# Twelve gather buffers instead of eight, and a tile's second eight gathers asked for earlier, in the first attention step of a four-layer graph kernel

## The chip, the cores and the metric

The kernel runs on one core of one Trainium2 chip. The metric is the device time of one execution in microseconds; the median of three executions is 3159.19 us. The engines are named as in the profile: PE is TensorE, DVE is VectorE, ACT is ScalarE, POOL is GpSimd, SP is SyncE. Each has a queue of its own that it works through in order.

## The reference

There are four layers over one graph of N = 4096 nodes with 256 features. Only layer 1 is touched here. Per step it forms attention weights, keeps of each row the largest ones that hold 90% of the mass, and multiplies the rows with them:

```
for n in range(STEPS):                       # STEPS = 2
    A = _top_p_attention(Xa, W1, W2, W3)     # softmax(q @ k.T), the smallest set of
                                             # largest entries with mass 0.9, renormalized
    Xf = R @ Xf                              # R: adjacency + identity, rows normalized
    Xa = A @ Xa
    Z = Z + Xf @ U1[n].T + Xa @ U2[n].T
h = X + Z                                    # then a layer norm
```

The layers around it are matrix products of the adjacency matrix with the features, small weights, and a layer norm after each.

## The kernel before, in words

The rows are cut into 32 tiles of 128. In step 0 the attention rows are sharp: nearly all rows need at most `KEPT = 16` of their 4096 entries. So the kernel does not multiply with a dense attention matrix there. For each tile it finds the 16 largest logits of every row and their columns (`tops`, with FIND_INDEX8 in two rounds of eight, L530), works out their weights (`pick`), and then fetches for k = 0 to 15 the feature row that the k-th column names: `gather` (L669) takes a buffer `G` of 128 x 256 float32 and issues an indirect DMA on POOL's queue, which reads 128 rows of 1 KB from `x1_d` in HBM. PE multiplies each `G` with a diagonal matrix `dg` of the k-th weights and sums the 16 products in `acc_bank` (L761). Rows for which 16 entries are not enough are flagged; `flag` (L582) works out a slot for each and writes the row's number into a list in HBM, `list_d`, with an indirect DMA of 128 elements of 4 bytes, on POOL's queue too (L606). They are done again later, densely.

`run_step` runs three tiles at once. In iteration i, tile i (`st`) is multiplied and finished, tile i + 1 (`cd`) is searched and gathered, and tile i + 2 (`nxt`) gets its logits. The body of an iteration is `pieces`: eight groups g = 0 to 7, each with a piece of the logits (L414), two of the 16 gather products of tile i (L761), four matmuls each of two products with the adjacency (`neighbours`: L686 into `acc_r`, L696 into `nef_ps`), and at the end the operations that `run_step` put into `ops[g]` with `at(g, ...)`. In the kernel before, the gathers of a tile are asked for in two halves:

- k = 0 to 7 by `run_step`, one iteration ahead, at the ends of groups 4 to 7 (two in each);
- k = 8 to 15 by `pieces`, in the tile's own iteration: directly after the product with k, the gather k + 8 is asked for.

With eight buffers in rotation, gather number s of the whole sequence takes the buffer of gather s - 8, so it waits on POOL until PE has multiplied with that one. For k = 8 to 15 this is the product with k - 8 of the same tile; for k = 0 to 7 of the next tile it is the product with k + 8 of this one.

Also on POOL's queue are the loads of the other copy of the adjacency, `adjn8` (L692), two of 256 KB in an iteration, each waiting for the matmuls L696 of an earlier half.

The order of the instructions on an engine is not the order of the Python text. The framework's planner plays the program through with costs of its own, takes for each engine the first instruction in text order that is ready in that play, and fixes the order so found; it also puts in the waits. It can be seen in the trace: in an iteration's start PE runs the products L761 of groups 0 to 2 and only then the eight L686 of groups 0 and 1, since `acc_r` is one buffer and is read first by `r_end` (L705 on ACT, L706 on DVE, behind a FIND_INDEX8 of 4.42 us). And `adjn8`'s load for the next iteration stands on POOL ahead of gathers that come earlier in the text.

Of the kernel before, what the change touches and what calls it, by code (L numbers as in the profile page):

```python
# [11 lines left out]
F32 = mybir.dt.float32  # L12
# [12 lines left out]
P = 128  # L25
D = 256
# [17 lines left out]
KEPT = 16  # L44
# [12 lines left out]
def gnn_stack(ctx, tc, x, adjt, adjn, w0, b0, w1, w2t, w3t, u1t, u2t, ln_g, ln_b, w2, b2, w3, b3, out):  # L57
# [28 lines left out]
    def half(bank):  # L86
        turns[bank] ^= 1
        return (mm_bank if bank == "mm" else acc_bank)[:, turns[bank], :]
# [268 lines left out]
    with tc.tile_pool(name="l1", bufs=1, reuse_waits="tile") as l1:  # L357

        cur = {"late": False, "n": 0, "nef_done": False}
# [57 lines left out]
        def logits_in(l):  # L417

            nc.vector.memset(l[:, N:], -1.0)
            return l  # L420
# [20 lines left out]
        def sparse(st):  # L441

            return cur["n"] == 0 and st["tile"] is not None
# [224 lines left out]

        def gather(st, k):  # L669

            st["G"][k] = g = cur["w"].tile([P, D], F32, tag="G", name="G", bufs=8)
            nc.gpsimd.indirect_dma_start(  # L672
                out=g, out_offset=None, in_=x1_d, in_offset=bass.IndirectOffsetOnAxis(ap=st["at"][:, k : k + 1], axis=0))

# [24 lines left out]
        def r_acc(i):  # L699

            return ps_acc.tile([P, 512], F32, tag=("acc", "nef")[i % 2 if cur["nef_done"] else 0], name="acc_r", bufs=1)
# [21 lines left out]
        def pieces(n, st, nxt, ops, rs_now=()):  # L723


            G = GP
            few = st is not None and sparse(st)
            if st is not None:
                e = st["e"]
                acc_a = half("acc")  # L730
                if "xf" not in st:
                    fetch(n, st)
            with_r = st is not None and len(rs_now) > 0
            if with_r:
                i, = rs_now
                acc_r, pn = r_acc(i), None
                if n == 0:
                    pn = ps_acc.tile([P, 512], F32, tag="nef", name="nef_ps", bufs=1)
            ats = {}

            def turn(g):
                ps = ps_tr.tile([P, 4, P], F32, tag="tr", name="at_ps")
                for j in range(G):
                    nc.tensor.transpose(ps[:, j, :], e[:, (g * G + j) * P : (g * G + j + 1) * P], ident)  # L744
                at = cur["w"].tile([P, G, P], F32, tag="at", name="at", bufs=2)
                ats[g] = at
                nc.scalar.copy(at[:, :G, :], ps[:, :G, :])  # L747

            if st is not None and not few:
                turn(0)  # L750
            for g in range(NLC):
                if nxt is not None:
                    logits_chunk(nxt["e"], nxt["q"], g)
                if few:
                    per = KEPT // NLC
                    for k in range(g * per, (g + 1) * per):
                        if k % 4 == 0:
                            dg = cur["w"].tile([P, 4, P], F32, tag="at", name="dg", bufs=2)
                            nc.vector.tensor_mul(dg, ident[:, None, :].to_broadcast([P, 4, P]),
                                                 st["w"][:, k : k + 4, None].to_broadcast([P, 4, P]))  # L760
                        nc.tensor.matmul(acc_a, dg[:, k % 4, :], st["G"][k], start=(k == 0), stop=(k == KEPT - 1))  # L761
                        if k + 8 < KEPT:
                            gather(st, k + 8)
                elif st is not None:
                    if g + 1 < NLC:
                        turn(g + 1)
                    for j in range(G):
                        jt = g * G + j
                        nc.tensor.matmul(acc_a, ats[g][:, j, :], cur["xa"][:, jt, :], start=(jt == 0),  # L769
                                         stop=(jt == NT - 1))  # L770
                if with_r:
                    neighbours(n, i, g, acc_r, pn, cur["xf"])
                for f in ops.get(g, ()):
                    f()
            if st is None:
                for i in rs_now:
                    r_product(n, i, cur["xf"])
            else:
                xa_new = work.tile([P, D], F32, tag="xa_new", name="xa_new", bufs=1)
                nc.scalar.activation(xa_new, acc_a, AF.Copy, scale=st["sc"])  # L780
                if n + 1 < STEPS:
                    put(xa_d, st, xa_new)
                st["xa"] = xa_new
            if with_r:
                r_end(i, acc_r, pn)
# [9 lines left out]
        def fetch(n, st):  # L795

            i = st["tile"]
            for key, src in (("xf", xf_d), ("res", h_d if n else x1_d), ("x1", x1b_d)):
                if n == 0 and (key == "x1" or key == "res" and i is not None):
                    continue  # L800
                if i is None:
                    st[key] = gathered(src, st, key)
                else:
                    st[key] = work.tile([P, D], F32, tag=key, name=key, bufs=1)
                    nc.sync.dma_start(st[key], rows(src, i))
            if n == 0 and i is not None:
                st["res"] = cur["xa"][:, i, :]
# [136 lines left out]
        def run_step(n, es):  # L944
# [37 lines left out]
            for i in range(-2, NT):  # L982
                st = tiles.pop(i, None)
                cd = tiles.get(i + 1)
                nxt = None
                if i + 2 < NT:

                    nxt = {"tile": i + 2, "q": cur["qs"].pop(0), "e": logits_in(es[i % 2]), "later": later, "G": {}}
                    tiles[i + 2] = nxt
                if i + 1 == NT and n == 0:  # L990
                    for fs in last:
                        for f in fs:
                            f()
                    last = []
                    left_over(n, es[NT % 2], later)
                ops = {}

                def at(g, f, *args):
                    ops.setdefault(g, []).append(lambda: f(*args))

                for g, fs in zip((1, 2), last):
                    for f in fs:
                        at(g, f)
                if 0 < i + 2 < NT - 1:
                    turned = []
                    g = 1 if n else 6
                    at(g - 1, lambda i, turned: turned.append(transposed(cur["xa"][:, i + 3, :])), i, turned)
                    at(g, lambda turned: cur["qs"].append(query(None, turned[0])), turned)
                if cd is not None:
                    peak_groups(cd, NG_LATER if n else ngr)  # L1010
                    at(1, exp_rows, cd)
                for job in jobs:
                    at(1, advance, job)
                if cd is not None:
                    rounds = ROUNDS if n else KEPT // 8
                    at(2, tops, cd, rounds)
                    at(2, pick, cd, rounds)
                    at(4, flag, cd)
                    if n == 0:
                        for k in range(8):  # L1020
                            at(4 + k // 2, gather, cd, k)
                    else:
                        at(5, lambda cd: [None for _ in settle(cd)], cd)
                for job in jobs:
                    if n and i + 1 == NT:
                        at(4, advance, job)
                    at(6, advance, job)
                if i + 1 == NT and n == 0:
                    cur["next"] = load_halves(es[1 - NT % 2], xf_d, nc.sync)
                if i < 0:  # L1030
                    now = FIRST[n][i + 2]
                else:
                    now = [i + 2] if FIRST[n][1][-1] < i + 2 < NT else []
                pieces(n, st, nxt, ops, now)
                last = [[f] for f in after(n, st)] if st is not None else []
                if i in starts:
                    k = starts[i]
                    if len(jobs) > (i == NT - 2):
                        last = finish(jobs.pop(0), last)
                    e = es[NT % 2] if k + 1 == LATER[n] else es[2]  # L1040
                    jobs.append({"stages": put_off(n, k, e, later)})
                    if i < NT - 2:
                        advance(jobs[-1])
# [28 lines left out]
        for n in range(STEPS):  # L1072
            cur["n"] = n
            with tc.tile_pool(name=f"step{n}", bufs=2, reuse_waits="tile") as cur["w"], \
# [6 lines left out]
                else:  # L1081
# [3 lines left out]
                    for c in range(NLC):  # L1085
# [5 lines left out]
                        k = kS[:, c * LC : (c + 1) * LC].rearrange("p (j d) -> p j d", d=P)  # L1091
# [137 lines left out]
```

## Time and profile before

| | |
|---|---|
| median of three executions (lowest, highest) | 3159.19 us (3156.39, 3160.6) |
| the profiled execution, its own time | 3226.1 us |
| its span, from first to last instruction | 3224.4 us |
| mean granted PE clock | 0.967 |
| step 0, gathers on POOL | from 388 us to 1314 us of the span |
| PE busy, whole span | 2945.7 us (91%) |
| POOL busy, whole span | 778.7 us (24%) |
| DVE busy, whole span | 2260.9 us (70%) |
| gathers (L672) | 512, mean 974 ns on POOL |
| list writes (L606), 400 us to 1400 us | 32, mean 1230 ns on POOL |
| FIND_INDEX8 (L530) | 64, mean 4419 ns on DVE |

How to read it: the profiled execution is one execution and took 67 us (2.1%) longer than the median of the others, so a difference taken from the trace is set against 3226.1 us first and then carried over to 3159.19 us. Shares over the whole span mix stages: POOL's 24% is mostly step 0. [...]

### The profile page before, as it was taken

Reading aid. Unit: us, or ns where it says so; the run is one execution under the profiler, and the core shown is the slowest. Engines: PE = TensorE matmul, PEld = TensorE weight load, DVE = VectorE, ACT = ScalarE, POOL = GpSimd, SP = SyncE. Lnnn points to the kernel's source line nnn. Section 1 sums busy time; section 2 is a strip of 40 time slices with the busy share of each in tenths; the row PEclk is TensorE's granted clock in tenths of the full one; section 3 lists DMA queues with packets and bytes.
Section 4 is the critical chain, followed back from the end, with each engine's and each line's share of the span. In section 5 each row is a group of like instructions: output and inputs, shape, how many; then the busy total and the mean of one; then the engine's idle time right before and its main releaser. Section 6 shows DMA issues by size and latency. Waiting matters only on the chain. (4 is left out here: it accounts for less than half of the span.)

```text
span 3224.4 us, 45413 instructions
## 1 busy us (share of the span) xinstructions
PE 2945.7 (91%) x14244; PEld 2313.2 (72%) x14244; DVE 2260.9 (70%) x7159; ACT 1729.6 (54%) x2883; POOL 778.7 (24%) x908
## 2 busy tenths in 40 slices
PE   7999888999989997779998999999999986999998
PEld 3788666777767775567777787778887654777886
DVE  4666667778777776447998898986999654444444
ACT  3555545556555554545554655555555434666664
POOL 1121256666666665100000000010000100000000
PEclk9999988999999998889999999999999997999999
DMA  9995467777777776241000011111111234333332
GB/s 169 157 178 121 82 96 121 140 140 138 139 134 138 134 135 135 88 122 38 24 24 23 27 37 32 32 35 33 38 34 29 85 108 143 107 108 97 107 107 79
DMA packets 247484, 299.44 MB, mean 93 GB/s; under 512 B 34464, under 2 KB 201312, under 8 KB 247232
## 3 DMA queue, kind: packets, MB, share of 16 engines
q0 software_dynamic: 46336, 104.28, 23.5%
q1 hardware_dynamic: 188656, 180.93, 18.7%
q10 hardware_dynamic: 12240, 11.23, 1.1%
q8 instruction: 115, 1.88, 0.3%
q14 instruction: 137, 1.12, 0.2%
HBM read 330.65 MB, written 66.32 MB: 123 GB/s over the span
## 5 line engine op out<-in xcount | busy, mean ns | idle before, releaser
L686 PE MATMUL acc_r<-xh,adjq 128*128 128x512 f32 x2048 | 619.3, 431 | 31.5 <-ACT adjq L683 17.1
L769 PE MATMUL acc_bank<-xa,at 128*128 128x256 f32 x2240 | 548.7, 385 | 26.8 <-ACT at L747 26.4
L672 POOL DMA_INDIRECT G<-x_d,cols x512 | 498.5, 974 | 296.1 <-PE acc_bank L761 143.3
L683 ACT CAST adjq<-adj 128x512 fp32r<-128x512 fp8e4 x512 | 316.4, 620 | 431.4 <-PE acc_r L686 237.2
L769 PEld LDWEIGHTS acc_bank<-xa,at 128*128 128x128 f32 x2240 | 408.3, 192 | 85.9 <-ACT at L747 38.1
L686 PEld LDWEIGHTS acc_r<-xh,adjq 128*128 128x128 f32 x2048 | 379.4, 191 | 125.8 <-ACT adjq L683 38.3
L433 DVE MAX8 cand<-e 128x8 f32<-128x228 f32 (+1 forms) x1088 | 387.3, 402 | 81.2 <-ACT e L415 44.8
L415 ACT COPY e<-lg 128x512 f32<-128x512 f32 x544 | 315.7, 586 | 209.2 <-PE lg L414 172.6
L199 POOL TENSOR_TENSOR rstd<-ve,mhalf 128x1 f32<-128x1 f32 x166 | 100.5, 606 | 1334.2 <-DVE ve L197 1274.0
L414 PE MATMUL lg<-kS,q 128*128 128x512 f32 x1088 | 391.9, 445 | 9.8 <-issue 5.5
L1109 ACT CAST a<-a 128x1024 fp32r<-128x1024 fp8e4 x256 | 268.4, 1050 | 167.0 <-PE acc L175 127.8
L761 PE MATMUL acc_bank<-G,dg 128*128 128x256 f32 x1024 | 291.8, 405 | 46.8 <-DMA G<-x_d,cols 15.1
L530 DVE FIND_INDEX8 cols<-top,e 128x8 uint32<-128x4096 f32 x64 | 282.8, 4419 | 0.0
L175 PE MATMUL acc<-xh,a 128*128 128x512 f32 x1024 | 262.1, 410 | 20.0 <-DMA x2i<-x_d 16.2
L761 PEld LDWEIGHTS acc_bank<-G,dg 128*128 128x128 f32 x1024 | 199.5, 200 | 104.5 <-issue 23.4
L175 PE MATMUL acc<-y0h,a 128*128 128x512 f32 x1024 | 249.8, 397 | 0.0
L175 PEld LDWEIGHTS acc<-xh,a 128*128 128x128 f32 x1024 | 193.3, 192 | 67.5 <-ACT xh L151 21.7
L175 PE MATMUL acc<-yh,a 128*128 128x512 f32 x1024 | 237.9, 394 | 0.0
L175 PEld LDWEIGHTS acc<-yh,a 128*128 128x128 f32 x1024 | 192.1, 188 | 43.8
L175 PEld LDWEIGHTS acc<-y0h,a 128*128 128x128 f32 x1024 | 187.9, 188 | 38.9 <-issue 0.6
L747 ACT COPY at<-at_ps 128x512 f32<-128x512 f32 x288 | 168.9, 588 | 82.4 <-PE at_ps L744 79.6
L414 PEld LDWEIGHTS lg<-kS,q 128*128 128x128 f32 x1088 | 182.3, 195 | 32.4 <-ACT e L415 11.1
(287 smaller groups left out, 4447.1 us busy)
## 6 DMA issues: line engine op xcount, KB each, us to landing
adj<-adj_d SPq DMA_DIRECT2D x256, 128.0 KB
a<-adj_d SPq DMA_DIRECT2D x256, 128.0 KB
a<-in_adjt POOLq DMA_DIRECT2D x64, 256.0 KB
adj_d<-a SPq DMA_DIRECT2D x64, 256.0 KB
adjn<-in_adjn POOLq DMA_DIRECT2D x64, 256.0 KB
x_d<-x SPq DMA_DIRECT2D x64, 128.0 KB
xf_d<-xf_new SPq DMA_DIRECT2D x64, 128.0 KB
G<-x_d,cols POOLq DMA_INDIRECT x512
```

The source lines that it names most:

```text
L175: nc.tensor.matmul(acc, a[:, j, :], halves(jt), start=(jt == 0), stop=(jt == NT - 1))
L414: nc.tensor.matmul(pl[:, :LC], q[k], kS[:, s], start=(k == 0), stop=(k == 1))
L415: nc.scalar.copy(l[:, s], pl[:, :LC])
L433: nc.vector.max(dst[:, 8 * g : 8 * g + 8], src[:, g * w : min((g + 1) * w, N)])
L530: nc.vector.max_index(st["at"][:, 8 * r : 8 * r + 8], t8, st["e"][:, :N])
L672: nc.gpsimd.indirect_dma_start(out=g, out_offset=None, in_=x1_d, in_offset=bass.IndirectOffsetOnAxis(ap=st["at"][:, k : k + 1], axis=0))
L683: nc.scalar.copy(a, cur["a8"][:, g % 2 * GP : (g % 2 + 1) * GP, :])
L686: nc.tensor.matmul(acc_r, a[:, j, :], xf[:, jt, :], start=(jt == 0), stop=False)
L747: nc.scalar.copy(at[:, :G, :], ps[:, :G, :])
L761: nc.tensor.matmul(acc_a, dg[:, k % 4, :], st["G"][k], start=(k == 0), stop=(k == KEPT - 1))
L769: nc.tensor.matmul(acc_a, ats[g][:, j, :], cur["xa"][:, jt, :], start=(jt == 0), stop=(jt == NT - 1))
L1109: nc.scalar.copy(a, a8)
```

## The change

The buffers of `G` become twelve. The gathers k = 8 to 15 of a tile leave the loop of products in `pieces`; `run_step` asks for them with `at` at the ends of groups 0 to 3 of the tile's own iteration, two in each group. The number of gathers, what they read and what is computed stay as they are. With twelve buffers in rotation, gather s takes the buffer of gather s - 12.

```diff
         def gather(st, k):
 
-            st["G"][k] = g = cur["w"].tile([P, D], F32, tag="G", name="G", bufs=8)
+            st["G"][k] = g = cur["w"].tile([P, D], F32, tag="G", name="G", bufs=12)
             nc.gpsimd.indirect_dma_start(
                 out=g, out_offset=None, in_=x1_d, in_offset=bass.IndirectOffsetOnAxis(ap=st["at"][:, k : k + 1], axis=0))
...
                         nc.tensor.matmul(acc_a, dg[:, k % 4, :], st["G"][k], start=(k == 0), stop=(k == KEPT - 1))
-                        if k + 8 < KEPT:
-                            gather(st, k + 8)
...
                         at(5, lambda cd: [None for _ in settle(cd)], cd)
+                if n == 0 and st is not None:
+                    for k in range(8, KEPT):
+                        at(k // 2 - 4, gather, st, k)
                 for job in jobs:
```

## The prediction, made before the changed kernel was run

> **What bounds the kernel now.** I read the page's groups first, then the busy times of 100 us stretches, then the waits, then the timelines of two iterations. The chain that ended last is of no use here: it begins at 2665.92 us, long after step 0.
>
> ```profile
> L672 POOL DMA_INDIRECT G<-x_d,cols x512 | 498.5, 974 | 296.1 <-PE acc_bank L761 143.3
> L761 PE MATMUL acc_bank<-G,dg 128*128 128x256 f32 x1024 | 291.8, 405 | 46.8 <-DMA G<-x_d,cols 15.1
> ```
>
> POOL waits for PE to free buffers (143.3 us), and PE waits for gathered rows (15.1 us of 46.8): each waits for the other, so the buffers are short or something delays the rows. The stretches inside step 0, with columns as named in their first line:
>
> ```profile
> core 0: us, PE busy (x) PEld busy (x) DVE busy (x) ACT busy (x) POOL busy (x), PEclk, DMA share, GB/s
> 700.00:800.00 100.00, 92.14 (x512) 72.04 (x513) 81.48 (x242) 58.17 (x114) 66.18 (x70) 1.00 0.77 146
> 800.00:900.00 100.00, 91.04 (x492) 71.61 (x492) 77.27 (x214) 59.20 (x116) 65.96 (x69) 0.97 0.80 133
> ```
>
> PE is the fullest engine and idle 8 us in 100. POOL is fuller than it looks: behind each of its 69 instructions lie 0.30 us in which it waits for nothing shown, so it is taken for 66 + 21 = 87 us. The waits from 500 to 1230 us (in total, times, longest):
>
> ```profile
> PE nef_ps L696 <- DVE spare_row L710: 26.9, 17, 3.5
> PE acc_bank L761 <- DMA G<-x_d,cols: 10.4, 9, 2.1
> PE acc_bank L761 <- issue: 7.7, 14, 4.4
> ...
> POOL G L672 <- PE acc_bank L761: 108.1, 108, 3.2
> ```
>
> Now one iteration, POOL's timeline and then PE's:
>
> ```profile
> 825.99 0.95 POOL L672 DMA_INDIRECT G<-x_d,cols  x1 [0.65 <-PE acc_bank L761]
> 827.24 1.36 POOL L606 DMA_INDIRECT list_d<-ids,slots  x1 [0.31 <-issue]
> 828.91 0.96 POOL L672 DMA_INDIRECT G<-x_d,cols  x1 [0.30 <-issue]
> ...
> 837.08 0.98 POOL L672 DMA_INDIRECT G<-x_d,cols  x1 [0.30 <-DMA list_d<-ids,slots]
> ```
> ```profile
> 833.93 1.13 PE L761 MATMUL acc_bank<-G,dg 128*128 128x256 f32 x4 [0.16 <-issue]
> ...
> 837.34 0.70 PE L761 MATMUL acc_bank<-G,dg 128*128 128x256 f32 x2 [1.11 <-DMA G<-x_d,cols]
> ```
>
> Counting the products L761 (two records each), 833.93 is k = 0 and 1 and 837.34 is k = 3. On POOL 825.99 is k = 2 of that tile, then comes the list write, then k = 3 at 828.91. So k = 3 is the first gather behind the list write, its rows were issued 8.4 us before PE got them, and POOL sees the list write end at about 837. The DMA view of 820 to 850 us (slices of 0.75 us) shows why:
>
> ```profile
> DMA  5051699999662090999636401489999999777062
> GB/s 202 5 164 34 161 278 98 101 96 265 219 183 64 0 120 5 38 44 60 27 22 44 27 22 33 112 273 358 153 109 138 284 358 389 290 150 255 29 178 49
> ```
>
> From the 15th to the 25th slice (831 to 839 us) mostly 22 to 60 GB/s move, and then at once 273 and 358: the list write holds up the gathers behind it for some 8 us, and a backlog follows. PE's other wait ends on the same event: the list write of 799.25 is followed by a stop that L710 shows, and of 15 such stops 13 end, with L710's start, 8.9 to 9.2 us after the list write.
>
> ```profile
> 799.25 1.37 POOL L606 DMA_INDIRECT list_d<-ids,slots  x1 [0.31 <-issue]
> ...
> 808.22 0.29 DVE L710 SCALAR_TENSOR_TENSOR spare_row<-nef_ps,ident 128x128 f32<-128x128 f32 x1 [2.68 <-remote]
> ```
>
> So a loop sets the pace: product k = 10 frees a buffer (852.0), 2.1 us later the list write issues (854.1; the buffer wait stands ahead of it), some 10.1 to 11.9 us after a list write product k = 3 starts (837.34 - 827.24 = 10.1, six other iterations 10.4 to 11.9), and from k = 3 to k = 10 PE needs 852.0 - 837.3 = 14.7 us. The sum, 26.9 to 28.7 us, is the period: L710 starts at 530.60 and 25 iterations on at 1226.02, 27.8 us each.
>
> **What the Trainium skill says.** "DMA: Bandwidth & Descriptors", section "Specifications": a transfer under 512 B costs a read-modify-write. The list write is 128 of 4 B, and the 22 to 60 GB/s agree. The same page, "SWDGE vs HWDGE vs iDMA": POOL's DMAs have one queue; the rows that come behind the list write agree. "Perfetto Trace Analysis", section "Optimization Strategy": the same gap repeating on the engine that should be full can mean too few buffers. The 108 waits of gathers on L761 agree, with the list write as the delay that the buffers fail to cover.
>
> **The change, part by part.** *Twelve buffers.* Gather s waits for product s - 12. Relative to the iteration that starts at 833.4, products k = 0 to 10 start at 0.5, 1, 2.2, 3.9, 6.4, 10.5, 12.6, 13, 15.6, 16, 18.6 us. With 1.25 us a gather (0.95 + 0.30), k = 12 to 15 issue at 1 to 6 us, and the next tile's k = 0 to 6 from 7 to about 20 us; its columns are there after the first FIND_INDEX8 (839.25, at 5.9 us). The list write has its slots when L600 is done on DVE (825.3, 18.7 us into its iteration). So six or seven gathers of the next tile stand ahead of the list write instead of three; the first behind it is k = 6 or 7, needed 12.6 us into the next iteration (39.5), while its rows come at about 20 + 11 = 31. The loop is cut with 8 us to spare. *The moved gathers.* Their count stays; POOL's work too: 16 x 1.25 + 1.66 (list write) + 2 x 0.9 (adjn8) = 23.5 us an iteration, below any period I expect. They pass the adjn8 loads and the list write on POOL; nothing of SP or PE moves. A gather that still waits for a product holds up the list write and adjn8 loads behind it; adjn8 has 11 to 14 us (849.08 issued, 860 used), the list write is read only at the step's end. I cost both at nothing; if that cover is gone, an adjn8 load late by one gather costs 1.25 us. *Four more KB per partition* cost no time. Bytes moved are the same.
>
> What goes, from 500 to 1230 us: PE's waits for G, 10.4 us, and its L761 waits "issue", 7.7 us, which lie at the same places (4.4 of it at 516.9 us, where the stage starts up). Of the stops at L710 (26.9 us, and 2.7 of the same kind booked as issue, together 29.6) the trace does not show what PE itself lacked: SP, ACT, DVE and POOL all resume at 808.2, as if PE's signals came late. If it was the rows, all 29.6 go; if the 4-byte writes slow the signals, or if it is the profiler's own traffic, none of it does. I take half, 14.8, with both ends for the range. Sum: 10.4 + 7.7 + 14.8 = 32.9 us in 26 iterations; 28 such iterations give 35.4. The last tile's products wait 1.85 + 0.65 + 0.37 = 2.9 us for rows at 1311 to 1314, which four free buffers cover. Total 38.3 us.
>
> What is late next: `acc_r`. From L688 (832.61) to the end of L706 behind the search (839.63) are 7.0 us, from L686 (841.43) to the next L688 (859.48) 18.05; that loop allows 25.1 us. PE's own work is about 24.4: five groups from 845.47 to 859.93, 14.5 us, three bare ones of 2.6, and 2.1 for the mix. So 38.3 us, a period of 26.5, is possible, and at most (27.8 - 25.1) x 28 = 76 us.
>
> From 3226.1 us this leaves 3187.8, a factor of 0.9881; from 3159.19 us, **3122 us**. With none of the stops gone (22 us) 3137, with all (54 us) 3105, at the bound 3084.
>
> **Rivals.** *The list write itself is the wait.* PE's stops are signals held up by its writes, and what k = 3 gains is lost there: the period falls by the waits for G alone, 10 us in all, 3149 us. For it: everything resumes at one moment. Against it: in the iteration of 833 PE ran on through the same 8 us. *The planner puts the list write early* (slower). In the text it stands before the next tile's gathers; what put three ahead of it was readiness in the planner's play. If at most one is ahead, k = 0 or 1 becomes the first behind it: list write at 18.7 plus 11 us is 29.7 where k = 0 is wanted at 27.4, a period of about 29.2, and (29.2 - 27.8) x 28 = 39 us lost, 3197 us. The point is between one and two gathers ahead (k = 2, wanted 2.2 us into the iteration, gives 27.5, no change). Against it: buffers come free earlier than before, so more should be ready, not fewer. *The gathers stay where the text has them*, in groups 0 to 3 and 4 to 7, with three ahead of the list write as now: no change, 3157 us.
>
> **How the numbers follow.** Forecast 0.70 (3084 to 3140), list write itself 0.11 (3140 to 3152), no change 0.06, slower 0.13. A measurement of this kernel can tell 0.2% (6.3 us) from no change, so faster 0.81, same 0.06, slower 0.13. The range is 3084 to 3151: it leaves out the slower case, most of no change and a little below the bound. The forecast's own range is 3084 to 3140.
>
> **What would show it.** Right: on POOL six or seven gathers of the next tile ahead of the list write; the waits of L672 on L761 down from 108 us to under 40; no L761 waiting for DMA; L710 at a period of 25.5 to 26.7. Half right: L710's stops still 9 us after the list write at 27 us in total. Wrong: fewer than three gathers ahead of the list write, or PE waiting for G at k = 0 to 2.

## The result, and the profile after

The changed kernel takes **3104.57 us** (median of five, 3101.93 to 3106.69), the kernel before beside it 3160.60 us (median of five, 3156.39 to 3169.46): ratio 0.9821, 95% interval 0.9806 to 0.9836, 56 us less. The profiled execution of the changed kernel took 3106.69 us, its span is 3105.0 us. The one of before had taken 3226.1 us, so between the two traces lie 119 us, twice the difference of the timed runs; the trace of before does not seem to belong with the timed runs, as is told below. Later groups of runs, each on another chip, gave 0.976 for the same change on one chip and 1.001 on another; that difference is half of what there is to learn here.

The two groups of the profile after (busy time, mean ns of one, idle time before and what ended most of it):

```profile
L672 POOL DMA_INDIRECT G<-x_d,cols x512 | 496.6, 970 | 214.4 <-PE acc_bank L761 77.6
L761 PE MATMUL acc_bank<-G,dg 128*128 128x256 f32 x1024 | 272.2, 387 | 12.5 <-DMA adj<-adj_d 5.4
```

PE's idle time before the products fell from 46.8 to 12.5 us, what is left is not for gathered rows, and a product takes 387 ns instead of 405. The same two stretches of step 0 as before, columns as in the first line:

```profile
core 0: us, PE busy (x) PEld busy (x) DVE busy (x) ACT busy (x) POOL busy (x), PEclk, DMA share, GB/s
700.00:800.00 100.00, 100.00 (x572) 80.07 (x571) 86.73 (x258) 64.40 (x126) 73.69 (x79) 1.00 0.84 153
800.00:900.00 100.00, 99.89 (x568) 79.89 (x567) 87.17 (x260) 64.75 (x128) 74.22 (x78) 1.00 0.86 152
```

PE is now busy all the time, so step 0's running part is at PE's pace. The start of L710 shows the period: from 582.86 to 1121.11 us, its ninth to its thirty-first start, lie 22 iterations of 24.47 us (27.73 in the trace of before, over the same 22). The waits from 500 to 1210 us (in total, times, longest):

```profile
POOL G L672 <- PE acc_bank L761: 72.3, 148, 2.1
PE acc_r L686 <- DVE xh L152: 8.9, 3, 7.8
PE acc_bank L761 <- DMA adj<-adj_d: 5.4, 1, 5.4
```

No product waits for G in this stretch; one wait of 3.7 us is left at 444 us, where the stage starts up. PE's waits listed here belong to the end of step 0, past 1150 us. POOL's timeline at one list write:

```profile
792.72 0.98 POOL L672 DMA_INDIRECT G<-x_d,cols  x1 [0.32 <-PE acc_bank L761]
794.00 0.95 POOL L672 DMA_INDIRECT G<-x_d,cols  x1 [0.30 <-PE acc_r L686]
795.71 0.94 POOL L672 DMA_INDIRECT G<-x_d,cols  x1 [0.76 <-PE acc_bank L761]
796.96 1.36 POOL L606 DMA_INDIRECT list_d<-ids,slots  x1 [0.30 <-issue]
```

The gather at 795.71 us starts 0.86 us after the products k = 10 and 11 did (PE, 794.85 us). With twelve buffers the gather that needs the buffer of k = 10 is k = 6 of the next tile: seven gathers (k = 0 to 6) of the next tile stand ahead of the list write, where it was three, and so it is in every iteration of the running part. The list write itself is as slow as ever. The DMA view of 790 to 820 us, in slices of 0.75 us:

```profile
DMA  8938979999750999099147426899999999967999
GB/s 329 294 118 130 198 93 122 115 132 294 225 177 21 55 71 27 0 82 57 25 34 33 18 22 148 245 307 246 101 131 229 350 413 373 336 227 163 252 130 101
```

From the 13th to the 24th slice, 799 to 808 us, it is 0 to 82 GB/s again. PE no longer notices.

### The profile page after: what moved, and what is told of

Same layout as the page of the kernel before. It is cut to its first block, busy times and chain, and to the rows that moved or that the text cites. A ratio compares the mean times of both kernels' runs of the same rounds, so it can differ in the third digit from the quotient of the medians.

```text
span 3105.0 us, 45412 instructions
## 1 busy us (share of the span) xinstructions
PE 2902.2 (93%) x14244; PEld 2300.0 (74%) x14244; DVE 2253.7 (73%) x7159; ACT 1725.0 (56%) x2883; POOL 779.8 (25%) x908
## 5 line engine op out<-in xcount | busy, mean ns | idle before, releaser
L767 PE MATMUL acc_bank<-xa,at 128*128 128x256 f32 x2240 | 548.1, 385 | 25.8 <-ACT at L747 25.4
L672 POOL DMA_INDIRECT G<-x_d,cols x512 | 496.6, 970 | 214.4 <-PE acc_bank L761 77.6
L767 PEld LDWEIGHTS acc_bank<-xa,at 128*128 128x128 f32 x2240 | 408.4, 192 | 84.3 <-ACT at L747 37.1
L415 ACT COPY e<-lg 128x512 f32<-128x512 f32 x544 | 315.0, 585 | 183.7 <-PE lg L414 179.9
L414 PE MATMUL lg<-kS,q 128*128 128x512 f32 x1088 | 385.0, 439 | 0.1
L761 PE MATMUL acc_bank<-G,dg 128*128 128x256 f32 x1024 | 272.2, 387 | 12.5 <-DMA adj<-adj_d 5.4
L761 PEld LDWEIGHTS acc_bank<-G,dg 128*128 128x128 f32 x1024 | 196.6, 193 | 49.5 <-DVE dg L759 10.0
L414 PEld LDWEIGHTS lg<-kS,q 128*128 128x128 f32 x1088 | 180.1, 192 | 20.4 <-ACT e L415 6.4
```

The lines of the kernel that those rows point to most:

```text
L414: nc.tensor.matmul(pl[:, :LC], q[k], kS[:, s], start=(k == 0), stop=(k == 1))
L415: nc.scalar.copy(l[:, s], pl[:, :LC])
L672: nc.gpsimd.indirect_dma_start(out=g, out_offset=None, in_=x1_d, in_offset=bass.IndirectOffsetOnAxis(ap=st["at"][:, k : k + 1], axis=0))
```

## Experiments

The runs were made in four groups; all kernels of a group, and the kernel before beside them, ran on one chip, and each group had another chip. I call them A (before: 3196.6 us), B (3198.33), C (3211.67) and D (3204.71). Times are compared within a group only. A period is the mean of 22 iterations in the kernel's own profile, from L710's ninth to its thirty-first start.

**Twelve buffers, nothing moved (chip A).** The kernel before with:

```diff
-            st["G"][k] = g = cur["w"].tile([P, D], F32, tag="G", name="G", bufs=8)
+            st["G"][k] = g = cur["w"].tile([P, D], F32, tag="G", name="G", bufs=12)
```

> The kernel before with twelve buffers for the gathered rows and nothing moved: the second eight gathers stay inside the pieces of the aggregation, behind product k - 8. Theory (the list write holds up the gathers behind it, and eight buffers put only three of the next tile's gathers ahead of it): in the steady state POOL's instructions have the same order with and without the move (three gathers, list write, five gathers, adjn8 load, eight gathers, adjn8 load); with twelve buffers the same places hold gathers that are four further on, so k = 7 is the first behind the list write. All of the gain comes with the buffers: ratio 0.982, about 3105 us, period of L710 24.4 us, no product waiting for its rows. Rival (the move is what brings the gathers out earlier): the buffers alone change nothing while the request for k + 8 still hangs on product k: ratio 1.00, 3155 to 3160 us, or about half of the gain, 3130 us, if both parts carry.

Measured: 3119.07 us, ratio 0.9755 (0.9721 to 0.9789), period 24.46 us. The buffers alone bring PE to its own pace: also here seven gathers stand ahead of the list write, without the move. The rival falls.

**The move alone (chip A).** The changed kernel with:

```diff
-            st["G"][k] = g = cur["w"].tile([P, D], F32, tag="G", name="G", bufs=12)
+            st["G"][k] = g = cur["w"].tile([P, D], F32, tag="G", name="G", bufs=8)
```

> The changed kernel with eight buffers again: only the move is left. Theory: gather k still waits for product k - 8 to free its buffer, wherever it stands in the text, and POOL's order is that of before: ratio 1.00 (0.998 to 1.002), about 3158 us; in the profile the period of L710 is 27 to 28 us, with stops 9 us behind each list write, three gathers of the next tile ahead of it, and a profiled execution some 60 us longer than the others, as the one of before was (3226.1 against 3160). Rival (the move carries the gain or half of it): ratio 0.982 to 0.991, 3105 to 3130 us. A gather that now stands ahead of an adjn8 load or the list write and holds it up would show as slower, up to 1.01.

Measured: 3199.84 us, ratio 1.0013 (0.9995 to 1.0031), period 27.30 us. The move does nothing that these runs can tell, and three gathers stand ahead of the list write as before. Its profile is also the eight-buffer profile of this chip, and it looks different from the one of before. PE's only waits between 480 and 1210 us:

```profile
PE acc_bank L761 <- DMA G<-x_d,cols: 59.9, 39, 4.1
```

The whole loss is named as waits for gathered rows; no stop shows at L710, which here starts 6.2 us behind the list write in 21 of 23 iterations. Where the waits fall speaks for the loop: between 560 and 1210 us 23 of 36 are at k = 3, the first gather behind the list write, and 11 at k = 4. And the profiled execution was not longer than the others (3198.1 us), so my expectation of 60 us more was wrong: profiling did not lengthen this kernel here.

**No list writes, eight buffers (chip A).** The kernel before; it leaves out the list writes of step 0 for all tiles but the last.

```diff
-            nc.gpsimd.indirect_dma_start(
-                out=list_d[cur["n"]], out_offset=bass.IndirectOffsetOnAxis(ap=at, axis=0), in_=rows_i, in_offset=None)
+            if cur["n"] or i == NT - 1:
+                nc.gpsimd.indirect_dma_start(
+                    out=list_d[cur["n"]], out_offset=bass.IndirectOffsetOnAxis(ap=at, axis=0), in_=rows_i, in_offset=None)
```

> The kernel before, eight buffers, with step 0's list write left out for all tiles but the last (rows that a tile flags for the later repair are not put on the list, so they would not be redone). Theory: without the 8 us in which the list write holds the queue, eight buffers are enough: PE paces at its own 24.4 us a tile, the stops that L710 shows are gone, no product waits for rows, ratio 0.982 to 0.984, 3104 to 3110 us; the profiled execution is within 10 us of the others. Rival (depth in general: eight buffers are too few whatever stands in the queue): the stops stay in part, ratio 0.99 to 1.00, 3130 to 3160 us. Rival (it is the POOL time of the list write, 1.66 us a tile, that counts): 28 x 1.66 = 46 us, 3113 us, which this run alone can't tell from the theory; the run with twelve buffers can.

Measured: 3282.81 us, ratio 1.0272 (1.0236 to 1.0308), which I did not expect. The stretches of its profile show two different things:

```profile
700.00:800.00 100.00, 100.00 (x567) 80.22 (x567) 88.19 (x263) 65.69 (x130) 69.03 (x74) 1.00 0.70 157
1800.00:2200.00 400.00, 207.78 (x1027) 170.72 (x1026) 379.39 (x850) 115.97 (x196) 15.18 (x20) 0.76 0.08 18
```

In step 0 PE is full with eight buffers, at a period of 24.43 us. But at 1800 to 2200 us PE is busy for only 208 us: the list of rows stays blank for all tiles but the last, and with it step 1's repair runs a search on DVE that the kernel before does not run (30 rounds of 4.49 us at L619 alone). For step 0 the theory holds: without the list write eight buffers are enough. It also refutes the rival that eight are too few whatever stands in the queue. The other rival, that it is the 1.66 us of POOL's own time that counts, falls with the run above: twelve buffers keep that time and reach the same pace.

**Nine buffers (chip A).** As the changed kernel with `bufs=9`.

> The changed kernel with nine buffers. Theory: one more buffer puts one more gather ahead of the list write (four, the first behind it is k = 4, whose product starts 2.5 us after that of k = 3). The loop of before, 26.9 to 28.7 us in the profiled execution and, from the 56 us that the change gained in 28 iterations, about 24.4 + 2.0 = 26.4 us in the others, falls by 2.5 us: 24 us, just under PE's own 24.4. So nine buffers give nearly all: ratio 0.982 to 0.986, 3105 to 3118 us; in the profiled execution, whose loop is longer, a period of 24.5 to 25.5. Rival (depth in general, each buffer giving a like part): a quarter of the gain, ratio 0.9955, 3146 us.

Measured: 3137.30 us, ratio 0.9815 (0.9782 to 0.9847), period 24.78 us. Four gathers now stand ahead of the list write, and 8 of the 9 waits for rows between 560 and 1210 us are at k = 4, again the first behind it. Its waits for rows between 480 and 1210 us:

```profile
PE acc_bank L761 <- DMA G<-x_d,cols: 19.0, 12, 3.4
```

One buffer of the four brings 59 of the 77.5 us. A gain of a like part for each (0.9955) is refuted: there is a threshold, and nine buffers lie next to it, as the loop said. Of the 18 us that they lose against twelve, the running part has 22 x (24.78 - 24.46) = 7; most of the rest lies behind it, where the last tiles' products wait for rows.

**The changed kernel again, and with ten buffers (chip B).**

> The changed kernel as it is, to stand beside the runs of this call and the one with twelve buffers and nothing moved (3119 us where the kernel before took 3197). Theory: the move adds nothing, so against the kernel before on the same chip it gives what twelve buffers alone gave, ratio 0.975 (0.972 to 0.979) if the kernel before takes about 3197 us, period 24.43 us. Rival (the move has a part of its own, in the first five tiles or the last): 5 to 15 us less than twelve buffers alone, ratio 0.971 to 0.974.

> The changed kernel with ten buffers. Nine gave a period of 24.73 us in the profile with 19.0 us of PE's waits for rows; ten put one more gather ahead of the list write (five; the first behind it is k = 5, 4 us after k = 4 in PE's order), and the loop falls to 21 to 22 us, well under PE's 24.4. Theory: as the change, period 24.43, within 5 us of it, ratio 0.975 to 0.979. Rival (depth in general): between nine and twelve, ratio 0.979, and waits for rows in most iterations.

Measured: the change 3119.11 us, ratio 0.9758 (0.9733 to 0.9783); ten buffers 3125.20 us, 0.9782 (0.9758 to 0.9806). The change gives what the buffers alone gave on chip A (0.9755); a part of its own for the move is not seen. With ten buffers five gathers stand ahead of the list write, and the period is 24.46 us, against 24.63 in the change's profile here, which has waits of 8.7 us for adjn8. The four times of ten buffers all lie above the four of the change, so the 6 us are real, but not from the running part. In the whole profile products wait 19.8 us for rows, 7.1 of it at 446 us, against 4.9 in the change's; which of it makes the 6 us isn't shown.

**The list write ahead of the next tile's gathers (chip B).** The prediction's slower rival as a kernel: the gathers' columns pass through two small DVE operations that depend on the tile's slots (in `flag`, ahead of the list write).

```diff
+            if sparse(st):
+                held = small("held", KEPT, mybir.dt.uint32)
+                none = small("none", 1, mybir.dt.uint32)
+                nc.vector.tensor_scalar(none, at.bitcast(mybir.dt.uint32), 0, None, op0=ALU.bitwise_and)
+                nc.vector.tensor_tensor(held, st["at"], none.to_broadcast([P, KEPT]), op=ALU.bitwise_or)
+                st["at"] = held
```

> The changed kernel, twelve buffers, with the columns of a tile's gathers passed through two small DVE operations that depend on the tile's slots (the values stay the same), so that on POOL the list write stands ahead of all of the next tile's gathers instead of behind seven of them. Theory, by the sum of the prediction's slower rival: slots at 18.7 us of an iteration, some 11 us from list write to rows, k = 0 wanted 0.5 us into the next iteration: period 18.7 + 11 - 0.5 = 29.2 us, against 27.3 of eight buffers on this chip and 24.4 of the change; 28 x 4.8 = 134 us over the change, about 3250 us, ratio 1.015 (1.00 to 1.03); PE waits for G at k = 0 to 2, once in each iteration. Rival (what counts is the number of buffers, wherever the list write stands): as the change, ratio 0.975 to 0.98.

Measured: 3311.89 us, ratio 1.036 (1.0334 to 1.0387), above the expected range, period 30.94 us, with twelve buffers. POOL's and PE's timelines at one list write (here the gather is L678, the list write L612, the product L767):

```profile
841.06 1.00 POOL L612 DMA_INDIRECT list_d<-ids,slots  x1 [3.13 <-DVE slots L600]
842.37 0.98 POOL L678 DMA_INDIRECT G<-x_d,held  x1 [0.30 <-issue]
```
```profile
846.13 1.02 PE L767 MATMUL acc_bank<-G,dg 128*128 128x256 f32 x4
...
852.02 2.05 PE L767 MATMUL acc_bank<-G,dg 128*128 128x256 f32 x4 [2.94 <-DMA G<-x_d,held]
```

From the list write to k = 0 are 10.96 us, the 11 of the rival's sum. The period is 1.7 us longer than its 29.2. In the iteration shown the slots come later: k = 0 had started at 819.93 us, and L600 began at 840.57, 20.6 us on instead of 18.2, because PE starts slow: the first four records after the wait take 2.05 us, four like them in the last busy stretch before it 1.02. No gather stands ahead of the list write now, and all waits for rows between 560 and 1210 us are at k = 0 (21) and k = 1 (10). So where the list write stands outweighs how many buffers there are.

**The same without list writes (chip B).** Leaves out the list writes as above.

> The run before with the list writes left out for all tiles but the last (as in the run without list writes, the list of rows for the later repair is then undefined, and the repair in step 1 runs a search of some 190 us more; only step 0 is to be compared). It has the late gathers but nothing that holds the queue. Theory: rows then come about 2.5 us after they are asked for; 18.7 + 3 + 2.5 = 24.2, so step 0 goes at PE's pace or just over it, 24.4 to 25.5 us a tile. Rival (the two DVE operations and the later request are what costs in the run before): the period stays at 28 to 29 us.

Measured: 3326.85 us, ratio 1.041 (1.0379 to 1.0441), with the longer repair in it; step 0 runs at 24.56 us a tile, with 2.9 us of waits for rows from 500 to 1150 us. The late requests and the two added operations by themselves cost at most the 0.1 us between this period and 24.46. It is the list write ahead of them that costs.

**The changed kernel a third time, and with a third adjn8 buffer (chip C).** The second has ten buffers for G and three for adjn8. It was meant for a stop of 5 us that the changed kernel shows near 500 us.

```diff
-            st["G"][k] = g = cur["w"].tile([P, D], F32, tag="G", name="G", bufs=12)
+            st["G"][k] = g = cur["w"].tile([P, D], F32, tag="G", name="G", bufs=10)
...
-                    cur["b8"] = cur["w"].tile([P, NT // 2, P], F8, tag="adjn8", name="adjn8", bufs=2)
+                    cur["b8"] = cur["w"].tile([P, NT // 2, P], F8, tag="adjn8", name="adjn8", bufs=3)
```

> The changed kernel a third time, to stand beside the next run on the same chip. 0.976 of the kernel before if the chip is like that of the runs so far, 0.982 if it is like that of the first comparison (3160.6 and 3104.57 us).

> Ten buffers for the gathered rows and three for adjn8 instead of twelve and two. Of the change, what is left of stops in step 0's running part is one of 4.6 to 5.3 us near 500 us, where an adjn8 load stands right behind a list write on POOL's queue and PE waits for it, and adjn8 waits of 2 to 4 us around 430 us. With a third adjn8 buffer the load of that tile is asked for ahead of the list write. Theory: the stop at 500 us and its slow products go, 5 to 8 us in all, and ten buffers cost at most the 2.8 us of waits for rows that the run with ten showed: 0 to 8 us less than the change on the same chip, ratio to it 0.997 to 1.000, too close for this comparison to be sure of. Rival (adjn8 isn't held by the list write but by its own 1 MB read at the DMA engines' limit): the stop stays wherever the load is asked for, and ten buffers cost up to 6 us: ratio to the change 1.000 to 1.002.

Measured: the change 3216.05 us beside 3211.67 of before, **ratio 1.0014** (0.9997 to 1.0031): on this chip it gains nothing. The other: 3208.06 us, 0.9985 (0.9967 to 1.0003), which is 0.9975 of the change, inside its expected 0.997 to 1.000, but not for the reason given: from 480 to 1210 us PE waits for adjn8 in neither profile, so nothing is settled on it. The expectation for the change was wrong, and its profile shows a stop that waits for no rows. PE's waits of the changed kernel on chip C from 480 to 1150 us:

```profile
PE nef_ps L696 <- DVE spare_row L710: 28.3, 16, 3.0
PE mm_bank L394 <- DVE slot L599: 8.4, 1, 8.4
PE mm_bank L820 <- issue: 5.4, 8, 2.1
```

No L761 waits for G, as the change promises, and yet the period is 27.28 us, with seven gathers ahead of the list write. One stop, all engines, behind the list write of 805.42 us:

```profile
805.42 1.35 POOL L606 DMA_INDIRECT list_d<-ids,slots  x1 [0.30 <-issue]
...
811.02 0.40 PE L696 MATMUL nef_ps<-adjn,adj 128*128 128x128 fp8e4 x4
...
814.39 0.29 DVE L710 SCALAR_TENSOR_TENSOR spare_row<-nef_ps,ident 128x128 f32<-128x128 f32 x1 [2.69 <-remote]
814.46 0.59 ACT L415 COPY e<-lg 128x512 f32<-128x512 f32 x1 [1.95 <-remote]
...
814.66 0.58 POOL L692 DMA_DIRECT2D adjn<-in_adjn  x1 [1.37 <-remote]
814.75 0.38 PE L696 MATMUL nef_ps<-adjn,adj 128*128 128x128 fp8e4 x4 [1.95 <-DVE spare_row L710]
```

L710 needs the matmul L696 of 811.02 us, done at 811.42. Here DVE, ACT and POOL all get going from 814.39 to 814.66 us, 9 us behind the list write, and PE then waits for L710. The change on chip B at the same place:

```profile
807.73 1.36 POOL L606 DMA_INDIRECT list_d<-ids,slots  x1 [0.30 <-issue]
...
813.35 0.40 PE L696 MATMUL nef_ps<-adjn,adj 128*128 128x128 fp8e4 x4
...
813.95 0.27 DVE L710 SCALAR_TENSOR_TENSOR spare_row<-nef_ps,ident 128x128 f32<-128x128 f32 x1
```

L710 starts 0.20 us after L696 ends. That is so in every profile of chips A and B and in the profile after: in each of L710's 23 starts it is 0.20 to 0.21 us. In the profile of before it is 1.25 to 4.55 us, in that of the change on chip C 1.26 to 4.37. So the trace of before is of chip C's kind, and the timed runs of the first comparison, to judge by the profile after, of the kind of A and B. On chips A to D the profiled execution is one of the timed ones; the one of before, 3226.1 us, is not, and of the times of the kernel before only chip C's (3198.32 to 3228.74 us) reach as far. It may have been taken on another chip than the 3159.19 us; the record doesn't say.

**The spare places spread out (chip D).** In `flag`, a row that needs no repair is written to a spare place of the list, and the spare places of the 128 partitions lie in 512 bytes side by side. This puts them 512 bytes apart; the rest stays, and so does the order on the engines.

```diff
-    list_d = [dram.tile([N + P, 1], I32, name=f"list{n}_d") for n in range(STEPS)]
+    list_d = [dram.tile([N + P * P, 1], I32, name=f"list{n}_d") for n in range(STEPS)]
...
-        nc.gpsimd.iota(spare, pattern=[[0, 1]], base=N, channel_multiplier=1, allow_small_or_imprecise_dtypes=True)
+        nc.gpsimd.iota(spare, pattern=[[0, 1]], base=N, channel_multiplier=P, allow_small_or_imprecise_dtypes=True)
```

> The kernel before (eight buffers, nothing moved) with the spare places of the lists, to which a tile's rows that need no repair are written, 512 B apart instead of 4 B apart. In the kernel before, the 128 writes of 4 B of a list write all go to the same 512 B, and in the traces the packets of both queues then take up to 6.9 us each, the hardware queue's too. Theory (the writes to one 512 B line are done one after the other and hold up all of the core's transfers, and on the chip of the last comparison also the signals between engines): spread out, the list write holds nothing for longer than a gather of 128 rows does; eight buffers are then enough, as they were without list writes (24.43 us a tile): ratio 0.970 to 0.985 to the kernel before on any chip, no stops 9 us behind the list write and no slices of 20 to 60 GB/s behind it. Rival (each 4 B write costs its time wherever it goes): no change, 0.998 to 1.002. Rival (the wider spread makes 128 separate read-modify-writes and is slower still): ratio 1.01 to 1.03.

> The changed kernel with the same spread of the spare places. Theory: PE's pace of 24.4 us a tile from the start of step 0, without the losses that remained near 430 and 500 us: the same time as the kernel before with the spread, or up to 10 us less, ratio to the kernel before 0.968 to 0.982 on any chip, so also on one like that of the last comparison, where the change alone gave 1.0014. Rival (each 4 B write costs its time wherever it goes): as the change alone on the same chip, 0.976 to 0.982 or 1.00.

Measured: 3167.75 us on the kernel before, ratio 0.9878 (0.9849 to 0.9906); 3169.51 us on the changed one, 0.9878 (0.9846 to 0.9911). The second lies above its expected range of 0.968 to 0.982 and the first, by a little, above its 0.970 to 0.985. The DMA view of the changed one from 790 to 820 us, with list writes at 793.97 and 819.73 us:

```profile
DMA  9899997403250756397899999726230643999999
GB/s 231 92 104 122 129 316 223 159 7 76 98 147 27 168 182 175 134 246 38 76 93 113 239 367 280 235 87 199 66 131 0 213 131 76 213 133 104 120 115 320
```

From 2 to 11 us behind the list write (796 to 805 us) 115 GB/s move on average, where the changed kernel of the first comparison has 37 (799 to 808 us). All profiles together say it more sharply. Between 560 and 1130 us there are 378 to 517 DMA packets that took over 2 us in each of the ten profiles with list writes as they were, up to 9.2 us, and none in the two without list writes (1.97 us at most) and in the two with the spread (1.97). So the hold is a matter of where the 4-byte writes go, not of their number or size. What is compared is profiles of different chips, as the spread ran on D alone; but the ten are of three chips and the first comparison, and agree. 37 and 35 us come off, with eight buffers and with twelve, and with eight no product waits for G from 480 to 1150 us though three gathers stand ahead of the list write. But PE's waits of the kernel before with the spread, in that stretch, still begin with the other stop:

```profile
PE nef_ps L696 <- DVE spare_row L710: 16.2, 11, 3.0
PE mm_bank L822 <- ACT xt L187: 12.5, 18, 2.1
```

The periods are 26.85 and 26.50 us, not 24.4. The expected "no stops 9 us behind the list write" failed: L710 starts up to 4.56 us after L696. The stop is therefore not, or not only, the held-up transfers. It became shorter, though: where ACT had waited for a logits matmul (L414) 7.5 to 10.5 us behind a list write, it started 2.5 us after it in the median on chip C (11 cases), and 1.0 us here (11 and 12). And it belongs to step 0: past 1350 us ACT's L415 starts 0.04 us after L414 on all four chips, some 37 times within 12 us of a list write of step 1, chip C's profile of the change included. So a list write alone, without step 0's gathers around it, did not bring the stop about.

## Why the prediction came out as it did

*The loop* (product k = 10, list write, k = 3, back to k = 10) was right on chips A and B; where the timed runs were made, the seven gathers and the absent waits of the profile after fit it. It said that the lead of gathers over the list write decides. None, three, four, five and seven gathers ahead of the list write gave 30.94, 27.30, 24.78, 24.46 and 24.46 us, with PE's waits, where there are any, mostly at the first gather behind it, and without the list write eight buffers were enough. *Six or seven gathers ahead* was right (seven). *The moved gathers at nothing* was right: the move alone is 1.0013 (0.9995 to 1.0031). *The adjn8 loads at nothing* failed once: near 500 us the changed kernel's PE waits 4.55 us for a load that POOL issued directly behind a list write.

*The size was off by 17 us* (3122 forecast, 3104.57 measured). The two traces seem to give the terms. The 7.7 us of L761 "issue" and the 10.4 us of waits are gone, as forecast. The stops at L710, "I take half, 14.8", are gone with all their 29.6 us, and for that case the prediction has 3105 (its own sum gives 3106). Slow products were left out altogether: PE's busy time is 2902.2 us after and was 2945.7, although its work is the same. But the two traces differ in kind as well as in kernel, and on chip C, within one kind, the change leaves the stops where they are (28.3 us). So the 29.6 us are not shown to be the change's work, and that 3105 comes so near to the measured time is luck. "What is late next: `acc_r`", 25.1 us, was wrong as a bound: the running period is 24.47. L688 to the end of L706 takes 6.0 us now (802.33 to 808.30) instead of the 7.0 that I read in an iteration with a disturbed start. "PE's own work is about 24.4" was right. The forecast period of 25.5 to 26.7 us was too long by 1.0 us at least.

*The sign "waits of L672 on L761 under 40 us" failed* (72.3): POOL asks as early as it can, so it waits in front of a bound PE too. Such a wait is no sign of too few buffers once PE has none.

*The step that held by luck is the transfer from the trace to the median.* I scaled a sum made in the profiled execution (3226.1 us) to runs 67 us shorter by a factor. That trace was of the kind of chip C: most of its loss showed as stops in which all engines resume together, and on chip C twelve buffers remove every wait for G and no time. There the rival "the list write itself is the wait" is what happens (it said 10 us less; measured 4 more, with an interval from 1 less to 10 more), and so is the prediction's sign of being half right, stops at L710 that stay at 27 us in total. On chips A and B the loss is all waits for rows, 59.9 us of them in 730 us, and twelve buffers take off 77.5 us (A, nothing moved) and 79.2 us (B). So the rival was not wrong, only not in force where the runs were timed. The argument against it, that PE ran on in the iteration of 833 us, was one iteration against 13 stops.

*What stays open.* What makes L710 and the others start so late on chips C and D; late signals of PE are one reading of it, not shown. That it sits 9 us behind the list write and that the spread shortens the kernel there speak for the list write; that stops remain with transfers flowing, and that step 1's list writes bring none, speak for something besides. A kernel without list writes was not run on such a chip, nor was the plain change on chip D, nor the spread on A or B. So the best version is not settled either: twelve buffers are best where they were tried alone on A and B, the spread with either number of buffers on D.

## What to carry to other kernels

Where an engine waits for gathered rows, look for the transfer in front of them in the same queue, and count how many requests stand ahead of it: here the lead that covers it had a threshold between three and five, and it is a matter of order as much as of buffers. Where a scatter (an indirect write) writes many small elements, look at whether they lie in one short stretch of memory, and try giving the ones that nobody reads places of their own. And before a sum is made from one trace, see whether that execution's time agrees with the timed ones; here it was 2% longer, and its waits were of another kind than those on chips A and B.

## What the hardware did that I had not expected

*Many 4-byte writes into the same 512 bytes hold up the core's transfers for some 8 us.* The Trainium skill, "DMA: Bandwidth & Descriptors", section "Specifications", puts the price on the size: under 512 B a read-modify-write. The runs put it on the place: with the same 128 writes of 4 B, 512 B apart, 115 GB/s move where 37 did, and no packet takes over 2 us. The prediction's reading of the page was too simple there. Which distance is enough was not tried.

*PE restarts at half speed.* "TensorE: Matmul & The Clock Gate", section "Part 1: The HAM clock gate", says that PE's clock falls to half after an idle window of some 3.4 us. In the run with the list write first, four records after a wait of 2.94 us took 2.05 us instead of 1.02; the granted clock is 0.50 from 851.4 to 858.2 us, and 0.88 to 0.95 in the stretches of 100 us from 500 to 1300 us. A stop costs more than its length. The wait was shorter than the page's window, which runs freely by its account. That fits the trace: the clock's changes at 820.68, 827.51, 851.40 and 858.23 us lie two and seven times 3.41 us apart. But in the 3.41 us before the fall at 851.40 PE was still busy until 849.07, so a wholly idle window was not needed here.

*The same change gains 2.4% on chip B and nothing on chip C.* On C and D, and in the trace of before, the DVE operation L710 starts up to 4.6 us after the matmul that it needs, in iteration after iteration of step 0; on A and B it starts 0.2 us after it.
